# Two tiles of a down product as 2x2 blocks with seven block products

## The chip, the cores and the metric

The kernel runs on one core of a Trainium2 chip. A core has TensorE (matmuls, which write to PSUM), VectorE, ScalarE and GpSimd (elementwise work) and SyncE, whose queue issues most DMAs. Each engine takes its instructions in the order of the program and waits at an instruction until what it needs is there. The metric is the device time of one execution in microseconds (us). In the profile PE is TensorE, DVE is VectorE, ACT is ScalarE, POOL is GpSimd and SP is SyncE.

## The reference

The input x has 2 x 2048 rows of 1024 numbers, all fp32. Each row is normalised, and two things are made of it: `s`, a sum of six rolled copies of the row, where the rolls are the six largest lags of its autocorrelation and the weights their softmax; and `g`, a gated feed-forward layer whose weights are tiled four times and carry a small low-rank (LoRA) part.

```python
xn = _layernorm(x)
corr = irfft(f * conj(f)), f = rfft(xn)
weights, delay = top_k(corr, 6)
s = sum over k of softmax(weights)[k] * roll(xn, -delay[k])
gate = silu(qlora(xn, w1q, a1, b1))          # 1024 -> 2752
up = qlora(xn, w3q, a3, b3)
g = silu(qlora(gate * up, w2q, a2, b2))      # 2752 -> 1024
out = x + s * g
```

Since w2q is tiled four times, gate * up can be summed over its four quarters first: 688 numbers per row, five chunks of 128 and a rest of 48.

## The kernel before

The 4096 rows are taken in eight macro blocks of 512 rows, each of four tiles of 128 rows. For a macro block the feed-forward layer is done in 15 steps, written out by hand (`plan`, L648). Steps 0 to 9 are the **up stage**: chunk c (two steps per chunk) has four quarters j, each with a gate and an up product of 512 columns into two PSUM accumulators (L544), seeded by ScalarE with the LoRA part (`seed`, L522, L515), then a Silu on ScalarE (L549), a multiply on VectorE (L551) and a sum over the quarters on GpSimd (L554, L556) into `zf[c]`. Step 10 is the rest (`up_rest`: L573 and L580, Silu L590, multiply L591, sums L595 to L597). Steps 11 to 14 are the **down stage**, one tile of 128 rows each: `down` multiplies the five chunks of `zf` with the two halves of w2 (512 columns each, L620), then adds a short product of 64 rows with the rest and the LoRA part (L631); `out` takes Silu (L642), multiplies with `s` (L643), adds x (L644) and stores (L645). `lora_mid` (L599) prepares the LoRA part of the short product in step 11 (L604).

Between these products the program puts the work of the correlation for the **next** macro block. `pre`, `mid`, `half` and `end` are lists of what is issued at four places of a step, and `sums` gives how many of the weighted rolled copies are added at two of them:

- norm of tile r (`norm`, L183) in steps 0, 2, 4, 6: ScalarE normalises, VectorE makes `a` and folds it (L192, L143, L144), GpSimd makes `b` and folds it (L194, L132, L133). `turn` (L206) transposes the folds on TensorE (L216) about two steps later.
- powers of the spectrum (`power`, L388) in steps 9 and 10: TensorE, then ScalarE copies and squares (L395, L396, L381), VectorE multiplies (L382), GpSimd adds (L383, L386).
- `lags` and `search` of tile r (L405, L435) in steps 11 to 14: TensorE (L414), ScalarE (L418, L432), VectorE (L425 to L449), GpSimd (L450).
- gathers: GpSimd issues an indirect DMA per rolled copy (L474), VectorE adds it with its weight into `s` (L491; the first of six is a ScalarE product, L488). In the settled blocks step 14 adds one, in the first block three.

PSUM accumulators of the products and of the down stage come from one pool of five (`full`, L93), handed out in turn: a new one is free when the readers of the one five before it have done. Other tiles in SBUF have one to three buffers per tag: `e2` and `o2` (squares) one each, `x2` (the x tile for the output) and `g` two each.

Of the kernel before, what the change touches and what calls it, by code (L numbers as in the profile page):

```python
# [35 lines left out]
F32 = mybir.dt.float32  # L36
# [5 lines left out]
L = 1024  # L42
# [5 lines left out]
P = 128  # L48
# [20 lines left out]
def block_kernel(ctx: ExitStack, tc: tile.TileContext, x, w13t, w0t, w5t, w2t, a13, b13, b5, a2t, tf, ti, pick, out):  # L69
# [12 lines left out]
    p5 = pool("p5", ROLLS)  # L82
    small = pool("small", 3)
# [23 lines left out]
    w2_sb = const.tile([P, NC, L], F32)  # L107
    b5_sb = const.tile([P, 4], F32)
# [20 lines left out]
    def fold_b(b, bcs):  # L129

        at = lambda first, par, n: bass.AP(b.tensor, b.offset + first, [list(b.ap[0]), [par, 2], [n, P]])
        nc.gpsimd.tensor_tensor(bcs[:, 0:2, :], at(0, 1, 2), at(512, -1, -2), ALU.subtract)  # L132
        nc.gpsimd.tensor_tensor(bcs[:, 2:4, :], at(2, -1, 2), at(510, 1, -2), ALU.add)  # L133
# [12 lines left out]
    def fold_lora(nat):  # L146

        pairs = p1.tile([P, 2, 8, 4], F32, tag="e2", name="a_pairs")
        nc.gpsimd.tensor_tensor(pairs, nat[:, 0], nat[:, 1], ALU.add)
        nc.gpsimd.memset(a13_sb, 0.0)  # L150
        whole = p1.tile([P, 8, 4], F32, tag="o2", name="a_whole")
        nc.gpsimd.tensor_tensor(whole[:, :2], pairs[:, 0, :2], pairs[:, 1, :2], ALU.add)
        nc.gpsimd.tensor_tensor(whole[:, 2:], pairs[:, 0, 2:], pairs[:, 1, 2:], ALU.subtract)
        nc.scalar.activation(a13_sb[:, :, :4], whole, AF.Copy, scale=0.125)


    class Corr:
# [25 lines left out]
        def norm(self, r, tags=("yc", "bcs")):  # L183
# [6 lines left out]
            yc = p1.tile([P, 4, P], F32, tag=tags[0], name=f"yc_{n}")  # L190
            bcs = p1.tile([P, 4, P], F32, tag=tags[1], name=f"bcs_{n}")
            nc.vector.tensor_tensor(a, xt[:, :512], xt[:, 512:], ALU.add)  # L192
            fold_a(a, yc, rest)
            nc.gpsimd.tensor_tensor(b[:, :512], xt[:, :512], xt[:, 512:], ALU.subtract)  # L194
# [43 lines left out]
        def lora_spread(self):  # L238
# [6 lines left out]
            self.u = p1.tile([P, NR], F32, tag="u", name=f"u_{self.m}")  # L245
# [79 lines left out]
        def lora_first(self, ffn):  # L325
# [3 lines left out]
            self.u = p1.tile([P, NR], F32, tag="u", name=f"u_{m}")  # L329
# [10 lines left out]
            for g, tags in enumerate((("ec", "e2"), ("zf2", "zf3"))):  # L340
                e = full(f"fe_{m}_{g}")
                self.wave(e, g, 0)
                ec, e2 = [p1.tile([P, NR], F32, tag=tag, name=f"{tag}_{m}_{g}") for tag in tags]
                nc.scalar.copy(ec, e)
                nc.scalar.activation(e2, e, AF.Square)
                parts.append((ec, e2))
# [7 lines left out]
            nc.vector.tensor_copy(self.u, acc)  # L354
# [19 lines left out]
        def squares(self, g, ec, e2, o):  # L374
# [5 lines left out]
            o2 = p1.tile([P, NR], F32, tag="o2", name=f"o2_{m}_{g}")  # L380
# [7 lines left out]
        def power(self, g):  # L388
# [4 lines left out]
            ec = p1.tile([P, NR], F32, tag="ec", name=f"ec_{m}_{g}")  # L393
            e2 = p1.tile([P, NR], F32, tag="e2", name=f"e2_{m}_{g}")
# [10 lines left out]
        def lags(self, r):  # L405
# [13 lines left out]
            corr = p1.tile([P, L], F32, tag="corr", name=f"corr_{n}")  # L419
# [74 lines left out]
    class Ffn:  # L494
# [114 lines left out]
        def down(self, r, mid, half):  # L609
            row = (self.m * RT + r) * P  # L610
            xs = []
            for d in range(2):
                xt = p2.tile([P, 512], F32, tag="x2", name=f"x2_{self.m}_{r}_{d}")
                nc.sync.dma_start(xt, x[row : row + P, d * 512 : (d + 1) * 512])
                xs.append(xt)
            accs = [full(f"y_{self.m}_{r}_{d}") for d in range(2)]
            rc = slice(r * P, (r + 1) * P)
            for d, acc in enumerate(accs):
                for c in range(FULL):
                    nc.tensor.matmul(  # L620
                        acc, lhsT=self.zf[c][:, rc], rhs=w2_sb[:, c, d * 512 : (d + 1) * 512], start=(c == 0), stop=False
                    )
                if d == 0:
                    if r == 0:
                        self.lora_mid()
                    mid()
                    half()

            for d, acc in enumerate(accs):
                at = slice(64 * d, 64 * d + 64)  # L630
                nc.tensor.matmul(  # L631
# [304 lines left out]
```

## Time and profile before

| | |
|---|---|
| median of three runs | 1165.69 us (1164.72 to 1165.73) |
| the profiled execution | 1167.36 us, span of its instructions 1165.6 us |
| mean granted TensorE clock | 0.994 |
| DMA | 201.78 MB, mean 173 GB/s |
| first down-stage matmul of the eight macro blocks | 144.9, 294.3, 433.9, 573.5, 713.1, 852.7, 992.3, 1118.2 us |

The profile is of one execution. Its parts are: busy time of each engine; groups of instructions by line, with the shape (partitions x elements), the count, the busy time, the mean duration of one in ns and the idle time of the engine before them with what ended it; timelines, with start and duration in us; and windows, which give the busy time of each engine in a stretch of time. A matmul in fp32 appears as two records that overlap, so its duration is not its pace; the distance between starts is. Idle time of an engine that is not the bound costs nothing.

### The profile page before, as it was taken

The numbers are of one execution on the slowest core, as the hardware profiler recorded it, in microseconds if no ns is written. First come the engines' busy times: TensorE is split into PE (matmuls) and PEld (weight loads), VectorE is DVE, ScalarE is ACT, GpSimd is POOL, SyncE is SP. The second block draws the span as 40 slices with busy tenths as digits, with TensorE's granted clock in tenths as the row PEclk, the third lists the DMA queues.
The fourth block names the chain that finished last, engine by engine and source line by source line (L and its number), as shares of the span: only waits on it lengthen the run. The fifth ranks groups of instructions, "written<-read, shape, count | busy, mean of one in ns | idle before, by whom it ended". The sixth has DMA issues, their size and how long they took to land.

```text
span 1165.6 us, 11210 instructions
## 1 busy us (share of the span) xinstructions
PE 1138.2 (98%) x3540; PEld 485.7 (42%) x3540; DVE 755.3 (65%) x1009; ACT 603.7 (52%) x1045; POOL 814.4 (70%) x675
## 2 busy tenths in 40 slices
PE   5999999999999999999999999999999999999997
PEld 4344344343444434444344433444344443444432
DVE  5587488665586746865577656785658765573455
ACT  4656623666346662566535664266633666344531
POOL 4778767877577884777767776787866877564653
PEclk9999999899999999999999999999999999999999
DMA  9941368534565435654355443754357534452334
GB/s 364 372 151 75 109 203 293 184 132 145 163 214 183 142 130 180 217 181 162 128 175 201 169 160 109 236 207 147 118 157 237 181 127 155 144 190 90 119 116 162
DMA packets 64915, 201.78 MB, mean 173 GB/s; under 512 B 7612, under 2 KB 7868, under 8 KB 64088
## 3 DMA queue, kind: packets, MB, share of 16 engines
q0 software_dynamic: 27648, 100.68, 26.9%
q1 hardware_dynamic: 37208, 100.39, 23.9%
q8 instruction: 28, 0.46, 0.2%
q14 instruction: 31, 0.25, 0.1%
HBM read 150.65 MB, written 50.39 MB: 172 GB/s over the span
## 4 chain that ended last, share of the span: by engine, by line
PE 87%; DVE 7%; POOL 2%; ACT 2%; issue 2%; DMA 0%; DVEq 0%; ACTq 0%; POOLq 0%
PE gu L544 44%; PE y L620 21%; PE u L527 4%; PE y L631 3%; PE gu L580 2%; PE t L216 2%; PE gu L573 2%; DVE s L491 1%; PE fe L369 1%; PE fe L372 1%; PE fo L369 1%; PE o L414 1%; PE fo L372 1%; PE ua L232 1%; PE e L414 1%
## 5 line engine op out<-in xcount | busy, mean ns | idle before, releaser
L544 PE MATMUL gu<-yT,w_sb 128*128 128x512 f32 x960 | 460.5, 601 | 0.1
L620 PE MATMUL y<-w_sb,zf 128*128 128x512 f32 x640 | 287.5, 597 | 0.5 <-ACT g L642 0.5
L544 PEld LDWEIGHTS gu<-yT,w_sb 128*128 128x128 f32 x960 | 176.8, 191 | 233.9 <-issue 214.4
L474 POOL DMA_INDIRECT roll<-scr,lag x192 | 230.2, 1199 | 47.4 <-issue 33.3
L491 DVE SCALAR_TENSOR_TENSOR s<-roll,w,s 128x1024 f32<-128x1024 f32 x160 | 249.0, 1556 | 7.2 <-DMA roll<-scr,lag 4.3
L551 DVE TENSOR_TENSOR z<-z,gu 128x512 f32<-128x512 f32 x160 | 109.2, 683 | 175.9 <-PE gu L544 118.0
L522 ACT ACTIVATE gu<-second,b_sb 128x512 f32<-128x512 f32 x320 | 207.6, 684 | 10.2 <-DVE z L551 9.3
L549 ACT ACTIVATE z<-gu 128x512 f32<-128x512 f32 x160 | 95.3, 596 | 177.8 <-PE gu L544 176.2
L620 PEld LDWEIGHTS y<-w_sb,zf 128*128 128x128 f32 x640 | 117.3, 190 | 147.8 <-issue 144.7
L644 POOL TENSOR_TENSOR g<-g,x 128x512 f32<-128x512 f32 x62 | 101.8, 1661 | 94.2 <-DVE g L643 88.5
L544 PE MATMUL gu<-yU,w_sb 128*128 128x512 f32 x320 | 163.8, 593 | 0.0
L556 POOL TENSOR_TENSOR zf<-zf,z 128x512 f32<-128x512 f32 x80 | 127.8, 1598 | 21.5 <-DVE z L551 20.3
L554 POOL TENSOR_TENSOR zf<-z,z 128x512 f32<-128x512 f32 x40 | 51.8, 1295 | 85.9 <-DVE z L551 84.2
L544 PEld LDWEIGHTS gu<-yU,w_sb 128*128 128x128 f32 x320 | 61.1, 191 | 77.2 <-issue 73.6
L643 DVE TENSOR_TENSOR g<-s,g 128x512 f32<-128x512 f32 x64 | 41.6, 690 | 67.5 <-ACT g L642 67.4
L450 POOL TENSOR_TENSOR e<-euler,e 128x6 f32<-128x6 f32 x32 | 45.8, 1431 | 41.8 <-DVE e L449 40.0
L642 ACT ACTIVATE g<-y 128x512 f32<-128x512 f32 x64 | 34.8, 593 | 77.3 <-PE y L631 59.6
L432 ACT COPY corr<-corr 128x511 f32<-128x511 f32 x32 | 19.8, 619 | 79.7 <-DVE corr L431 79.7
L527 PE MATMUL u<-z,a_sb 128*2 128x512 f32 (+1 forms) x384 | 52.9, 591 | 2.0 <-DVE z L551 2.0
L143 DVE SCALAR_TENSOR_TENSOR yc<-a,rest 128x256 f32<-128x256 f32 x28 | 41.6, 1487 | 5.3 <-POOL rest L188 2.0
L515 ACT ACTIVATE gu<-second,b_sb 64x512 f32<-64x512 f32 x64 | 43.9, 686 | 1.7
L418 ACT COPY oc<-o 128x258 f32<-128x258 f32 x32 | 12.0, 375 | 63.0 <-PE o L414 62.8
(167 smaller groups left out, 1358.9 us busy)
## 6 DMA issues: line engine op xcount, KB each, us to landing
scr<-x SPq DMA_DIRECT2D x64, 512.0 KB
x<-in_x SPq DMA_DIRECT2D x32, 512.0 KB
x<-in_x SPq DMA_DIRECT2D x64, 256.0 KB
out<-g SPq DMA_DIRECT2D x64, 256.0 KB
w_sb<-in_w13t SPq DMA_DIRECT2D x5, 1024.0 KB
second<-rows SPq DMA_DIRECT2D x14, 256.0 KB
w_sb<-in_w2t SPq DMA_DIRECT2D x1, 3072.0 KB
roll<-scr,lag POOLq DMA_INDIRECT x192, 5.7
```

What stands on the lines that cost most here:

```text
L450: nc.gpsimd.tensor_tensor(e, bass.AP(euler.tensor, euler.offset, [list(euler.ap[0]), [0, TOP]]), e, ALU.pow)
L474: nc.gpsimd.indirect_dma_start(out=g, out_offset=None, in_=st.scratch[r].rearrange("p (n o) -> (p n) o", o=1), in_offset=bass.IndirectOffs ...
L491: nc.vector.scalar_tensor_tensor(s, g, w, s, ALU.mult, ALU.add)
L522: nc.scalar.activation(acc, self.st.second[:, wi, :], AF.Copy, scale=b13_sb[:, c, q : q + 1])
L527: nc.tensor.matmul(self.u2[32 * j : 32 * j + 2, :], lhsT=a2_sb[:rows, 4 * c + j, :], rhs=z[:rows, :], start=(c == 0), stop=(c == FULL),)
L544: nc.tensor.matmul(acc, lhsT=w13_sb[:, c, 2 * j + wi, k, :], rhs=y, start=False, stop=(k == 1), skip_group_check=True,)
L549: nc.scalar.activation(z, accs[0], AF.Silu)
L551: nc.vector.tensor_tensor(z, z, accs[1], ALU.mult)
L554: nc.gpsimd.tensor_tensor(self.sum_of(c), zs[0], zs[1], ALU.add)
L556: nc.gpsimd.tensor_tensor(self.zf[c], self.zf[c], z, ALU.add)
L620: nc.tensor.matmul(acc, lhsT=self.zf[c][:, rc], rhs=w2_sb[:, c, d * 512 : (d + 1) * 512], start=(c == 0), stop=False)
L644: (nc.vector if last else nc.gpsimd).tensor_tensor(g, g, xs[d], ALU.add)
```

## The change

Two tiles (i = 0, 1; `q` counts the pairs) are taken together in the down stage. The first four chunks of `zf` are named by two numbers: chunk 2a + k. The product of a pair over these chunks is one of 2x2 blocks: rows i, inner index k, column halves n, where each block product is a sum over a (two matmuls). A scheme after Strassen and Winograd makes it from seven block products instead of eight:

- Once, in the first macro block, GpSimd forms four combinations of w2 (`mix_weights`, 1024 elements each): T1 (in place of a block of w2), T2, T3, T4.
- Per macro block GpSimd forms four combinations of `zf` for a = 0 at the end of step 8 and for a = 1 at the end of step 9 (`mix`): S1, S2, S4 in buffers of the norm (`a`, `yc`, `bcs`) and A10 replaced in place by A00 - A10.
- A pair takes two steps. `down_head` makes p1, copies it on ScalarE into a second accumulator, makes p7, copies that to SBUF, adds p6 to p1, and VectorE writes p1 + p6 + p7 to a third; then p2 and the plain chunk 4. `down_tail` adds p5, VectorE writes that plus p7 to the fourth, and p4, p3, the plain chunks and the short products follow. All four accumulators are held from the head on. Outputs of the first half are issued in the middle of the tail.
- In `norm` the subtraction for `b` and both its folds go from GpSimd to VectorE.
- `px`, a pool of three buffers under one tag `x2`, holds the squares `e2` and `o2`, the x tiles of the output, and the finished output, which is now written over the x tile. The fourth x tile of a pair is loaded after the first output. `ec` goes to the two `g` buffers, `corr` to that of `cT`, `u` to that of `us`.
- The sums of rolled copies are dealt out anew: step 12 one instead of three, step 14 three instead of one (settled blocks); in the first block similar. The seeds of the next macro block move to the middle and the end of the last step.

```diff
     def fold_b(b, bcs):
...
-        nc.gpsimd.tensor_tensor(bcs[:, 0:2, :], at(0, 1, 2), at(512, -1, -2), ALU.subtract)
-        nc.gpsimd.tensor_tensor(bcs[:, 2:4, :], at(2, -1, 2), at(510, 1, -2), ALU.add)
+        nc.vector.tensor_tensor(bcs[:, 0:2, :], at(0, 1, 2), at(512, -1, -2), ALU.subtract)
+        nc.vector.tensor_tensor(bcs[:, 2:4, :], at(2, -1, 2), at(510, 1, -2), ALU.add)
...
+    B = lambda k, n: w2_sb[:, :4, :].rearrange("p (a k) l -> p a k l", k=2)[:, :, k, n * 512 : (n + 1) * 512]
+    T1, T2, T3, T4 = B(0, 1), t_sb[:, 0], t_sb[:, 1], t_sb[:, 2]
+    mix_weights = [
+        lambda: nc.gpsimd.tensor_tensor(T3, B(1, 1), B(0, 1), ALU.subtract),
+        lambda: nc.gpsimd.tensor_tensor(T1, B(0, 1), B(0, 0), ALU.subtract),
+        lambda: nc.gpsimd.tensor_tensor(T2, B(1, 1), T1, ALU.subtract),
+        lambda: nc.gpsimd.tensor_tensor(T4, B(1, 0), T2, ALU.subtract),
+    ]
...
             nc.vector.tensor_tensor(a, xt[:, :512], xt[:, 512:], ALU.add)
+            nc.vector.tensor_tensor(b[:, :512], xt[:, :512], xt[:, 512:], ALU.subtract)
             fold_a(a, yc, rest)
-            nc.gpsimd.tensor_tensor(b[:, :512], xt[:, :512], xt[:, 512:], ALU.subtract)
             fold_b(b[:, :], bcs)
...
-            o2 = p1.tile([P, NR], F32, tag="o2", name=f"o2_{m}_{g}")
+            o2 = px.tile([P, NR], F32, tag="x2", name=f"o2_{m}_{g}")
...
+        def mix(self, a):
...
+            S1, S2, S4 = [t[:, 2 * a : 2 * a + 2, :] for t in self.S]
+            A = lambda i, k: self.zf[2 * a + k].rearrange("p (q i n) -> p q i n", q=2, i=2)[:, :, i, :]
+            nc.gpsimd.tensor_tensor(S1, A(1, 0), A(1, 1), ALU.add)
+            nc.gpsimd.tensor_tensor(S2, S1, A(0, 0), ALU.subtract)
+            nc.gpsimd.tensor_tensor(A(1, 0), A(0, 0), A(1, 0), ALU.subtract)
+            nc.gpsimd.tensor_tensor(S4, A(0, 1), S2, ALU.subtract)
...
+        def down_head(self, q, mid, half):
...
+            for i, n in ((0, 0), (1, 0), (0, 1)):
+                self.load_x(i, n)
...
+                    (A(0, 0), B(0, 0)), (A(0, 1), B(1, 0)), (S[2], B(1, 1)), (A(1, 1), T4), (S[0], T1), (S[1], T2), (A(1, 0), T3),
...
+            self.ys = [full(f"y_{self.m}_{2 * q + i}_{n}") for n in range(2) for i in range(2)]
+            y00, y10, y01, y11 = self.ys
+            self.add_to(y01, p1_, True)
+            nc.scalar.copy(y00, y01)
+            self.add_to(y11, p7_, True)
+            self.p7 = p5.tile([P, NR], F32, tag="z", name=f"p7_{self.m}_{q}")
+            nc.scalar.copy(self.p7, y11)
+            self.add_to(y01, p6_)
+            nc.vector.tensor_tensor(y10, y01, self.p7, ALU.add)
+            if q == 0:
+                self.lora_mid()
+            mid()
+            half()
+            self.add_to(y00, p2_)
+            self.add_to(y00, self.plain(0, 0))
+
+        def down_tail(self, mid, half, s, between):
...
+            self.add_to(y01, p5_)
+            nc.vector.tensor_tensor(y11, y01, self.p7, ALU.add)
+            mid()
+            half()
+            self.add_to(y10, p4_)
+            self.add_to(y10, self.plain(1, 0))
+            self.rest(0, (y00, y10))
+            self.out(0, 0, y00, s)
+            self.load_x(1, 1)
+            self.out(1, 0, y10, s)
+            between()
+            self.add_to(y01, p3_)
+            self.add_to(y01, self.plain(0, 1))
+            self.add_to(y11, self.plain(1, 1))
+            self.rest(1, (y01, y11))
+            self.out(0, 1, y01, s)
+            self.out(1, 1, y11, s)
...
+            (nc.vector if last else nc.gpsimd).tensor_tensor(xt, g, xt, ALU.add)
+            nc.sync.dma_start(out[row : row + P, cols], xt)
...
-        sums[8], sums[9], sums[11], sums[14] = (2, 1), (2, 1), (1, 0), (1, 0)
+        sums[7:10] = [(2, 1)] * 3
+        sums[11:] = [(1, 0), (1, 0), (2, 1), (3, 0)]
+        between = lambda: None
         if first:
-            sums = [(0, 0)] * 7 + [(1, 1), (2, 1), (1, 1), (2, 2), (2, 2), (2, 1), (2, 1), (3, 0)]
+            sums = [(0, 0)] * 7 + [(1, 1), (2, 1), (1, 2), (2, 2), (2, 1), (1, 0), (2, 1), (3, 0)]
+            for p, f in enumerate(mix_weights):
+                half[6 + p].append(f)
...
-            mid[STEPS - 1].insert(0, lambda: (ffn_next.seed(0), ffn_next.seed(1, (0,))))
+            mid[STEPS - 1].insert(0, lambda: ffn_next.seed(0, (0,)))
+            between = lambda: (ffn_next.seed(0, (1,)), ffn_next.seed(1, (0,)))
             end[STEPS - 1].insert(0, lambda: ffn_next.seed(1, (1,)))
+        for a in range(2):
+            end[8 + a].append(lambda a=a: ffns[m].mix(a))
```

## The prediction

> **What bounds the kernel now.** I read the page first (busy shares), then TensorE's own waits, then one macro block (rows 1536 to 2047, the fourth) engine by engine. TensorE is the bound nearly everywhere:
>
> ```profile
> PE 1138.2 (98%) x3540; PEld 485.7 (42%) x3540; DVE 755.3 (65%) x1009; ACT 603.7 (52%) x1045; POOL 814.4 (70%) x675
> ```
>
> A busy TensorE need not be a fast one, so I looked at the pace. Each fp32 matmul of 128x512 appears as two records, and inside a run of them the starts are 0.429 us apart: ten records of L620 start at 573.48 and the next ten at 585.27 and so on, always 4.46 us for ten. One matmul is 0.858 us. Three groups, and the windows of the down stage (573.5 to 617.4) and of the following up stage (busy us of TensorE, its weight loads, VectorE, ScalarE, GpSimd; then the granted clock):
>
> ```profile
> L620 PE MATMUL y<-w_sb,zf 128*128 128x512 f32 x640 | 287.5, 597 | 0.5 <-ACT g L642 0.5
> L386 POOL TENSOR_TENSOR bT<-bT 128x1024 f32<-128x1024 f32 x8 | 19.8, 2469 | 0.6
> L383 POOL TENSOR_TENSOR bT<-e,o 128x512 f32<-128x512 f32 x16 | 20.3, 1270 | 3.0 <-ACT o L381 2.5
> ```
>
> ```profile
> 573.50:617.40 43.90, 43.90 (x137) 19.54 (x135) 29.80 (x46) 12.72 (x23) 26.12 (x20) 1.00 0.59 190
> 617.40:713.10 95.70, 95.70 (x301) 39.57 (x300) 62.72 (x79) 62.80 (x108) 75.51 (x65) 1.00 0.47 160
> ```
>
> To be seen: in a settled macro block (139.6 us from one to the next) TensorE has no idle time at all. Whatever the others take is hidden today; the question is only whether it stays so. TensorE's real waits are few: 9.2 us at the start, then 1.2, 2.0, 1.9, 0.5 and 2.6 us, all before 210 us.
>
> **What is removed.** Per macro block the old down product takes 40 matmuls of 128 rows; the new one takes, per pair of tiles, seven products of two matmuls and four plain ones, 36 in all. The short ones (L631) stay 8, in the same concurrent pairs. Eight blocks x 4 x 0.858 = **-27.5 us**, wholly on TensorE's path.
>
> **What is added off TensorE, costed by rows.** Per pair: two ACT copies (L395, a copy out of PSUM, 0.58 us) and two VectorE adds with a PSUM operand (L551, 0.68 us): 19 and 22 us over the kernel. Per half block `mix` puts four 256-element adds on GpSimd. No row shows that size undisturbed; 512 elements take 1.27 (L383) and 1024 some 2.4 (L386), so a straight line gives 0.7, with the 0.08 us between dependent adds 0.8, **3.2 us** per `mix`; ends 2.5 (half of 1.27 each) and 4.1 (L133 beside a busy VectorE, 1.03). I take 3.2. Against that the fold of b leaves GpSimd: 1.28 + 0.91 + 1.03 = 3.2 us x 28 = 90 us less. On VectorE it costs 0.69 + 0.42 + 0.42, but a and yc, now 0.69 + 1.51 + 1.07 beside the GpSimd folds, should fall to the 0.69 + 0.50 + 0.42 of the first block's undisturbed rows, so VectorE's norm goes from 3.3 to 3.1 us. As sums none of this binds. But four new orders are laid across queues, and each has to be checked where it sits.
>
> **Wait 1, start of the down stage.** Before, tile 0 needed one free accumulator at once and one 4.4 us later. Now the first product goes to the third accumulator allotted (`y01`), which is the one of the second group of the rest (`gu_5_1`) and is free only after its VectorE multiply (L591). The timelines of GpSimd, ScalarE, VectorE and TensorE before that point:
>
> ```profile
> 550.70 1.27 POOL L554 TENSOR_TENSOR zf<-z,z 128x512 f32<-128x512 f32 x1 [1.30 <-DVE z L551]
> 556.26 1.27 POOL L556 TENSOR_TENSOR zf<-zf,z 128x512 f32<-128x512 f32 x1 [1.29 <-DVE z L551]
> 559.38 3.21 POOL L386 TENSOR_TENSOR pwy<-pwy,cT 128x1024 f32<-128x1024 f32 x1
> 566.31 1.28 POOL L556 TENSOR_TENSOR zf<-zf,z 128x512 f32<-128x512 f32 x1
> 567.53 1.26 POOL L383 TENSOR_TENSOR bT<-e,o 128x512 f32<-128x512 f32 x1
> ...
> 569.33 0.59 ACT L381 ACTIVATE o<-fo 128x512 f32<-128x512 f32 x1
> ...
> 570.67 1.30 DVE L591 TENSOR_TENSOR z<-z,gu 64x512 f32<-64x512 f32 x2
> ...
> 573.48 4.46 PE L620 MATMUL y<-w_sb,zf 128*128 128x512 f32 x10
> ```
>
> Today L591's second ends at 571.97, 1.5 us before it would be needed. The first `mix` comes after the add at 550.70, the second after the one at 566.31. GpSimd's idle time between takes part of the first: L386 starts 0.9 late. The second is in full, so the add at 567.53 ends at 573.1 instead of 568.8. Of the shared tag `x2` (three buffers) the last square `o2` takes the buffer that this add frees, and ScalarE runs in order: `o2` starts at 573.1 instead of 569.33, and behind it are queued the four Silu of the rest, then the copies of the LoRA rows, then the new copy of `y01`. L591's second ends 2.64 us after `o2` starts, at 575.8: TensorE waits up to 2.3 us. With the cheap end of `mix` it is 1.1; I take **2.1 us** x 6 blocks = +12.6. The last block has no powers and waits for nothing here. In the first block the four weight sums (1024 elements, 2.4 us each) lie on GpSimd too, and there L591's second already ends 3.3 us after the point where TensorE would now need it (148.2 against 144.9): I take 4.5, less the 1.9 us wait of the short product there, which goes because that product moves back: **+2.6**.
>
> **Wait 2, inside the down stage.** The product into `y01` must wait until VectorE has read it twice. The first reading has 3 us of room. The second (`y11`) is queued behind a search (3.0 us), up to two gather sums (1.28 each) and a lag fold (0.95), and the search comes late by what delayed GpSimd. Laying VectorE's rows in order from 576 gives `y11` ready within 0.2 us of need for the first pair and 0.5 us late for the second. Ends 0 and 2; I take **0.6** x 7 = +4.2.
>
> **Wait 3, start of the next up stage.** The last step now has three sums ahead of the output multiplies. A Silu needs one of two `g` buffers, which GpSimd's add frees, so the last two Silu, the multiplies, the search and then L551 move back; the last x tile is loaded only when the first output has left its buffer, (on SP that load waits for the first store to land, and the second store behind it), and GpSimd stands at its add with the power of the next weights and `rstd` behind it, for which ScalarE's norm waits. The first block already ends with three sums, so the row is there: its successor starts at 192.45 and its first L551 at 201.84, 9.4 us after, against 4.85 us in the settled block; and the transposes stall:
>
> ```profile
> 209.01 0.66 PE L216 MATMUL t<-ident,yc 128*128 128x128 f32 x2 [2.56 <-DVE yc L143]
> 209.91 0.69 PE L216 MATMUL t<-ident,yc 128*128 128x128 f32 x2 [0.24 <-DVE yc L144]
> ...
> 622.32 0.68 DVE L551 TENSOR_TENSOR z<-z,gu 128x512 f32<-128x512 f32 x1
> ...
> 631.31 0.60 PE L216 MATMUL t<-ident,yc 128*128 128x128 f32 x4
> ```
>
> In the settled block the last fold of b ends at 631.07, 0.2 us ahead of the transposes, so there is no room. Ends 0 and 2.8, the measured stall. The norm in one queue ends 0.9 us sooner than 4.0 us (627.04 to 631.07); the x load gives back about half a us. I take **2.4** x 6 = +14.4, the first boundary having its stall already.
>
> **Ends.** The last output waits for its late x tile: about +0.6.
>
> **The clock.** The trace shows what an idle TensorE costs afterwards:
>
> ```profile
> 92.60:96.00 3.40, 1.45 (x5) 0.34 (x5) 3.30 (x8) 3.40 (x7) 2.21 (x4) 1.00 0.00 0
> 96.00:99.40 3.40, 3.40 (x11) 2.31 (x10) 3.36 (x6) 1.78 (x4) 2.11 (x2) 0.50 0.00 0
> 154.00:157.40 3.40, 1.88 (x5) 0.57 (x3) 3.26 (x5) 0.00 (x0) 2.27 (x3) 1.00 1.03 308
> 208.60:215.50 6.90, 6.25 (x13) 3.29 (x14) 5.85 (x9) 4.09 (x9) 6.63 (x6) 0.51 0.56 179
> ```
>
> An idle 1.95 us was followed by 3.4 us at half clock (1.7 us lost), 2.56 us by 6.8 us (3.4 lost), one of 1.87 us, cut by the edge of a 3.4 us stretch, by none. The Trainium skill ("TensorE: Matmul & The Clock Gate", the part on HAM oscillation) says instead that only idle gaps over about 3.4 us let the clock fall. By that rule waits of 2.1 and 2.4 us cost nothing more; by the rows each may cost 1.7 to 3.4. The rows decide; since the stretch is cut at times that don't follow the kernel, and a slow TensorE shortens the next wait, I take three falls of 1.7: **+5.1**.
>
> **Sum.** -27.5 + 12.6 + 2.6 + 4.2 + 14.4 + 0.6 + 5.1 = **+12.0**. The profiled execution took 1167.36 us (span 1165.6 and 1.8 around it), so it would be 1179.4; it lies 1.7 above the median of the runs, 1165.69, so for the runs I say **1178**. Without the clock it is 1173.
>
> **Rivals.** (1) *The waits stay hidden.* If `mix` costs 2.5 and GpSimd, 90 us lighter, has caught up, wait 1 is 0.7, wait 2 nothing, wait 3 0.7: 4.2 + 1.5 + 4.2 + 0.6 = 10.5 us against 27.5, so **1149**; 1140 to 1158. For it: GpSimd's 26 us of 43.9 in the down stage and VectorE's 30. It decides if the second `mix` ends before about 569.5. Against it: GpSimd has no idle time from 559.4 to 577.8. Chance 0.27. (2) *Gain and waits cancel*, 1163 to 1168: 0.09. (3) *The clock falls at every wait*: 13 waits at up to 3.4 us, 44 us in place of 5.1: **1217**; 1192 and more. For it the row at 208.6; against it the one at 154. Chance 0.12. That fewer matmuls are not fewer TensorE microseconds I leave out: the pace is even. My own case has 0.52, 1166 to 1192.
>
> **Numbers.** Measurement tells about 0.2% (2.3 us) from no change. Faster: rival 1 and a little of mine, 0.28; within 0.2%: 0.09; slower: 0.63. A tenth left out at each end, in rivals 1 and 3, gives 1147 to 1200.
>
> **What would show it.** L620's successors with 576 records of 0.429 us; idle time of TensorE before the first of them in each down stage, released by VectorE's multiply; GpSimd's add of the third power ending some 4 us later against TensorE; idle time before the first transposes; clock windows at 0.5 after them. I am wrong if the block period is under 138 us: then `mix` was absorbed, or the accumulators come free in another order than I counted.

## The result and the profile after

The changed kernel takes **1177.14 us** (median; 1176.3 to 1179.55) against 1165.71 for the kernel before beside it: ratio 1.0103, 95% interval 1.0085 to 1.012. The profiled execution has a span of 1177.7 us against 1165.6, so 12.1 us have to be found, and with the 27.5 us of matmuls that are gone, 39.6 us of something new.

In the changed kernel the first block deals out only 22 of its 24 sums of rolled copies. Every later block then runs two places behind in the list: its fourth tile is stored before its last two copies are added, and the last two of all are never added. Every run below on the changed kernel has this too, unless its text says that it has 24. The prediction did not see it. What it is worth in time is measured below, with the late load of x out of the way (`x4_24`); for the changed kernel as it stands it was not measured.

First the page: busy time of each engine (us, share of the span, instructions) and the groups that bear on the change (busy us, mean ns of one, then idle time ahead of them and what ended it).

```profile
PE 1120.5 (95%) x3476; PEld 472.5 (40%) x3476; DVE 758.2 (64%) x1122; ACT 619.5 (53%) x1077; POOL 779.3 (66%) x659
...
L503 DVE SCALAR_TENSOR_TENSOR s<-roll,w,s 128x1024 f32<-128x1024 f32 x158 | 237.1, 1501 | 17.5 <-DMA roll<-scr,lag 14.9
...
L724 POOL TENSOR_TENSOR x<-g,x 128x512 f32<-128x512 f32 x62 | 84.9, 1379 | 72.2 <-DMA x<-in_x 46.4
L641 PE MATMUL y<-w_sb,zf 128*128 128x512 f32 x256 | 121.4, 596 | 0.0
...
L641 PE MATMUL y<-t_sb,zf 128*128 128x512 f32 x128 | 64.0, 624 | 5.7 <-DVE z L603 5.7
...
L641 PE MATMUL y<-w_sb,S 128*128 128x512 f32 x128 | 61.9, 606 | 2.0 <-DVE y L698 2.0
```

The product has its 576 records (256 + 128 + 128, and 64 more of another operand), TensorE 64 fewer in all: 32 matmuls are gone as counted. But at `L724`, the add of x, GpSimd has stood idle 46.4 us for loads of x. In the kernel before the same add had 5.5:

```profile
L644 POOL TENSOR_TENSOR g<-g,x 128x512 f32<-128x512 f32 x62 | 101.8, 1661 | 94.2 <-DVE g L643 88.5 <-DMA x<-in_x 5.5
```

Now the windows of one settled block, its down stage and the up stage after it (busy us of TensorE, its weight loads, VectorE, ScalarE, GpSimd; then the granted clock):

```profile
583.00:624.65 41.65, 41.04 (x129) 17.88 (x127) 31.97 (x53) 16.61 (x31) 25.73 (x20) 1.00 0.58 187
624.65:724.25 99.60, 97.49 (x300) 40.61 (x299) 60.73 (x89) 60.88 (x105) 67.99 (x61) 0.98 0.47 159
```

From its first product to the first of the up stage the down stage became shorter, 43.99 us (573.48 to 617.47) to 41.65. The up stage, whose products nobody touched, went from 95.6 to 99.6 us, with 2.1 us of idle TensorE and a clock of 0.98. So the loss lies behind the product, not in it. TensorE's waits over the whole execution (us in total, times, longest):

```profile
PE t L230 <- DVE yc L145: 15.2, 6, 3.0
...
PE y L641 <- DVE z L603: 5.7, 1, 5.7
PE y L641 <- ACT y L681: 3.6, 6, 0.6
```

The first row is the transposes at the start of the up stage, the second the new product p7 in the first block, the third the new product p6 in six settled blocks. Smaller ones, 2.0 us at L641 for the add L698 and 1.8 at L426, lie in the first block. Put against the prediction's terms (sums of the trace's waits and of the time at half clock, the stretch after the last matmul left out of the latter; a stretch at half clock counts half):

| term | predicted | measured |
|---|---|---|
| matmuls removed | -27.5 | -27.5 |
| start of the down stage, settled blocks | +12.6 | +3.6 (6 x 0.61) |
| waits in the first block | +2.6 | +8.7 (5.2 to 13.9, the transposes after it included) |
| inside the down stage | +4.2 | 0 in settled blocks |
| start of the up stage | +14.4 | +12.5 (2.20, 2.99, 2.11, 2.69, 2.50) |
| end, after the last matmul | +0.6 | +3.5 (6.8 to 10.35) |
| clock | +5.1 | +6.8 (10.2 us at half clock before, 23.9 after) |
| waits before the first block's down stage | 0 | +1.6 |
| rest, in no wait; 0.5 us a settled down stage are starts further apart | 0 | +2.9 |
| sum | +12.0 | +12.1 |

The sum is right and its parts are not; the experiments ask why.

**Start of the down stage.** The timeline of GpSimd, ScalarE, VectorE and TensorE (start, duration, engine and line; in brackets idle time before and its releaser):

```profile
580.07 0.72 POOL L636 TENSOR_TENSOR S<-zf,S 128x256 f32<-128x256 f32 x1
580.75 1.26 POOL L395 TENSOR_TENSOR bT<-e,o 128x512 f32<-128x512 f32 x1
...
582.05 0.60 ACT L393 ACTIVATE o<-fo 128x512 f32<-128x512 f32 x1 [3.25 <-POOL bT L395]
582.54 2.03 ACT L602 ACTIVATE z<-gu 64x512 f32<-64x512 f32 x4
...
586.78 0.57 ACT L681 COPY y<-y 128x512 f32<-128x512 f32 x1
...
583.40 2.52 DVE L603 TENSOR_TENSOR z<-z,gu 64x512 f32<-64x512 f32 x4
...
583.01 1.88 PE L641 MATMUL y<-w_sb,zf 128*128 128x512 f32 x4
584.84 1.96 PE L641 MATMUL y<-t_sb,zf 128*128 128x512 f32 x4
587.40 1.98 PE L641 MATMUL y<-t_sb,S 128*128 128x512 f32 x4 [0.61 <-ACT y L681]
```

The chain is there link by link: `mix` (last add L636), the held add L395, the square L393 that waits 3.25 us for it, the Silu and the multiply L603, whose second instruction ends at 583.40 + 2 x 0.63 = 584.66. But the product that needs it is p7, at 584.84, and not p1, which starts at 583.01, before the first of these multiplies. So it comes 0.2 us in time, and the one wait left is p6 for the copy of `y01` at the end of ScalarE's queue.

**Start of the up stage**, same block (SPq is SyncE's queue):

```profile
626.65 0.34 SPq L725 DMA_DIRECT2D out<-x  x1
630.79 0.33 SPq L659 DMA_DIRECT2D x<-in_x  x1
...
634.06 1.27 POOL L724 TENSOR_TENSOR x<-g,x 128x512 f32<-128x512 f32 x1 [4.32 <-DMA x<-in_x]
635.29 1.35 POOL L462 TENSOR_TENSOR e<-euler,e 128x6 f32<-128x6 f32 x1
636.63 0.54 POOL L191 TENSOR_TENSOR rstd<-var,mhalf 128x1 f32<-128x1 f32 x1
...
637.57 1.24 ACT L200 ACTIVATE x<-x,shift,rstd 128x1024 f32<-128x1024 f32 x1 [3.09 <-POOL shift L193]
...
640.15 0.48 DVE L145 SCALAR_TENSOR_TENSOR yc<-a,rest 128x256 f32<-128x256 f32 x1
...
640.77 1.06 PE L230 MATMUL t<-ident,yc 128*128 128x128 f32 x4 [2.11 <-DVE yc L145]
```

SyncE issues the store of the first output at 626.65 and the load of the fourth x tile only at 630.79, when that store has left the buffer (in SyncE's waits, `SPq L659 <- DMA out<-x: 54.5, 25, 3.9`: 54.5 us in 25 loads). GpSimd stands 4.32 us at its last add for this tile, with the power for the softmax weights (L462) and `rstd` of the next norm (L191) queued behind; ScalarE's norm waits 3.09 us for those, VectorE's folds for the norm, and the transposes 2.11 us for the folds.

**Clock.** Windows right after the transposes' waits of 2.99 and 2.11 us, and then after that of 2.50 us; the clock is the third number from the end:

```profile
500.90:504.20 3.30, 3.30 (x5) 1.24 (x4) 3.30 (x4) 2.15 (x6) 3.13 (x2) 0.50 0.42 158
640.90:644.20 3.30, 3.30 (x11) 2.26 (x12) 3.30 (x7) 2.63 (x6) 1.82 (x1) 0.50 0.94 322
924.70:928.00 3.30, 3.30 (x14) 1.76 (x15) 3.30 (x7) 2.82 (x7) 1.75 (x1) 1.00 0.91 320
```

The wait of 2.69 us is like the first two, that of 2.20 us like the last. So three waits were followed by 3.41 us at half clock, two by none.

### The profile page after: what moved, and what is told of

Same layout as the page of the kernel before. It is cut to its first block, busy times and chain, and to the rows that moved or that the text cites. A ratio compares the mean times of both kernels' runs of the same rounds, so it can differ in the third digit from the quotient of the medians.

```text
span 1177.7 us, 11263 instructions
## 1 busy us (share of the span) xinstructions
PE 1120.5 (95%) x3476; PEld 472.5 (40%) x3476; DVE 758.2 (64%) x1122; ACT 619.5 (53%) x1077; POOL 779.3 (66%) x659
## 4 chain that ended last, share of the span: by engine, by line
PE 50%; POOL 19%; DMA 11%; issue 9%; ACT 6%; DVE 4%; SPq 0%; POOLq 0%; DVEq 0%; ACTq 0%
PE gu L556 37%; POOL roll L486 5%; DMA x<-in_x 5%; DMA out<-x 4%; PE y L641 3%; POOL x L724 3%; PE u L539 3%; PE t L230 2%; DMA roll<-scr,lag 2%; POOL e L462 2%; ACT gu L527 2%; POOL bT L395 1%; POOL zf L568 1%; PE fe L381 1%; PE fo L381 1%
## 5 line engine op out<-in xcount | busy, mean ns | idle before, releaser
L486 POOL DMA_INDIRECT roll<-scr,lag x192 | 240.1, 1250 | 51.4 <-issue 30.5
L503 DVE SCALAR_TENSOR_TENSOR s<-roll,w,s 128x1024 f32<-128x1024 f32 x158 | 237.1, 1501 | 17.5 <-DMA roll<-scr,lag 14.9
L724 POOL TENSOR_TENSOR x<-g,x 128x512 f32<-128x512 f32 x62 | 84.9, 1379 | 72.2 <-DMA x<-in_x 46.4
L641 PE MATMUL y<-w_sb,zf 128*128 128x512 f32 x256 | 121.4, 596 | 0.0
L566 POOL TENSOR_TENSOR zf<-z,z 128x512 f32<-128x512 f32 x40 | 57.9, 1447 | 85.8 <-DVE z L563 85.7
L462 POOL TENSOR_TENSOR e<-euler,e 128x6 f32<-128x6 f32 x32 | 46.7, 1461 | 69.0 <-DVE e L461 69.0
L723 DVE TENSOR_TENSOR g<-s,g 128x512 f32<-128x512 f32 x64 | 55.2, 885 | 39.0 <-ACT g L722 37.6
L641 PEld LDWEIGHTS y<-w_sb,zf 128*128 128x128 f32 x256 | 46.9, 191 | 57.9 <-issue 57.0
L641 PE MATMUL y<-t_sb,zf 128*128 128x512 f32 x128 | 64.0, 624 | 5.7 <-DVE z L603 5.7
L641 PE MATMUL y<-w_sb,S 128*128 128x512 f32 x128 | 61.9, 606 | 2.0 <-DVE y L698 2.0
L206 DVE TENSOR_TENSOR a<-x 128x512 f32<-128x512 f32 x28 | 33.1, 1183 | 26.7 <-ACT x L200 26.7
```

The source lines that it names most:

```text
L462: nc.gpsimd.tensor_tensor(e, bass.AP(euler.tensor, euler.offset, [list(euler.ap[0]), [0, TOP]]), e, ALU.pow)
L486: nc.gpsimd.indirect_dma_start(out=g, out_offset=None, in_=st.scratch[r].rearrange("p (n o) -> (p n) o", o=1), in_offset=bass.IndirectOffs ...
L503: nc.vector.scalar_tensor_tensor(s, g, w, s, ALU.mult, ALU.add)
L566: nc.gpsimd.tensor_tensor(self.sum_of(c), zs[0], zs[1], ALU.add)
L641: nc.tensor.matmul(acc, lhsT=lhs, rhs=rhs, start=(first and a == 0), stop=True, skip_group_check=True)
L724: (nc.vector if last else nc.gpsimd).tensor_tensor(xt, g, xt, ALU.add)
```

## The experiments

Times are medians; each ratio is to the kernel before, run beside it, with its 95% interval. All edits are to the changed kernel, except `fold_only`. The question was what delays the transposes: the three sums of the last step (my weightier reason) or GpSimd standing for the late x tile (in my working "about half a us").

### x4_early: the fourth x tile loaded early

```diff
# down_head, after the first products
+            self.load_x(1, 1, p5, "z")
# down_tail, after the first output
-            self.load_x(1, 1)
```

> The changed kernel with the fourth x tile of a pair loaded already in the head, into a buffer of the z tag that is free then, instead of after the first output. Theory A (the three sums of step 14 make the search late, and GpSimd's wait for x is only the last 1.1 us of it): the waits before the first transposes fall from 2.1 to 3.0 us to about 1.0 to 1.9, no clock falls there, the end of the kernel is 3.5 us shorter; about 1161 us. Theory B (GpSimd's 4.3 us wait for x, with the power and rstd behind it, makes the whole wait): the waits are gone; about 1155 us.

Measured: 1158.12 us, ratio 0.9939 (0.9915 to 0.9962). The same place in its timeline:

```profile
619.34 1.27 POOL L724 TENSOR_TENSOR x<-g,x 128x512 f32<-128x512 f32 x1 [0.68 <-issue]
622.16 1.35 POOL L462 TENSOR_TENSOR e<-euler,e 128x6 f32<-128x6 f32 x1 [1.54 <-DVE e L461]
...
625.33 1.24 ACT L200 ACTIVATE x<-x,shift,rstd 128x1024 f32<-128x1024 f32 x1 [1.93 <-POOL shift L193]
...
628.53 0.69 PE L230 MATMUL t<-ident,yc 128*128 128x128 f32 x4 [0.36 <-DVE yc L145]
```

GpSimd no longer waits for x, but for the search; the transposes wait 0.35 to 0.39 us instead of 2.1 to 3.0, the clock falls after none of them, and five settled blocks take 138.1 us each instead of 141.2 in the mean. The stretch after the last matmul goes from 10.35 to 8.6 us. With the three sums still in place, 0.36 us is all that they and everything else leave: the late x tile was the cause. (The edit also takes this tile out of the shared pool of three buffers; the run does not separate that from the earlier load.)

### sums_back: the sums where the kernel before had them

```diff
-        sums[11:] = [(1, 0), (1, 0), (2, 1), (3, 0)]
+        sums[11:] = [(1, 0), (2, 1), (2, 1), (1, 0)]
```

> The changed kernel with three sums in step 12 and one in step 14 in the settled blocks, as the kernel before has them. Theory A: the waits before the first transposes are gone in the five settled blocks, with the falls of the clock there, the end stays; about 1160 us. Theory B: the waits stay at 2.1 to 3.0 us; about 1177 us. In both VectorE could reach the first reading of y01 of the second pair late, by up to 1.3 us a block.

Measured: 1184.47 us, ratio 1.0161 (1.0135 to 1.0187). The transposes' waits went to between 0 and 0.8 us in the settled blocks, but not because the norm came sooner: the x add comes 53.7 us after the block's first product instead of 51.1. TensorE itself comes later. Two products inside the down stage now wait in every block like this:

```profile
616.90 1.98 PE L641 MATMUL y<-w_sb,S 128*128 128x512 f32 x4 [1.29 <-DVE y L686]
625.43 1.98 PE L641 MATMUL y<-w_sb,S 128*128 128x512 f32 x3 [2.02 <-DVE y L698]
```

These are the adds that turn `y01` into `y10` and `y11`. They stand on VectorE behind the sums that moved, the second also behind 1.7 us in which VectorE waits for the first, scaled copy of a tile on ScalarE (L500); TensorE waits 0.3 to 1.3 us and 2.0 us. That is the prediction's wait 2, and the place of the sums in the changed kernel is what keeps it away.

### mix_late: the second mix later

```diff
-        for a in range(2):
-            end[8 + a].append(lambda a=a: ffns[m].mix(a))
+        end[8].append(lambda: ffns[m].mix(0))
+        mid[10].insert(0, lambda: ffns[m].mix(1))
```

> The changed kernel with the second mix of a block issued in the middle of step 10, before the fourth power, so that GpSimd adds the third power first. If the wait of 0.6 us before p6 comes from o2 waiting for GpSimd behind that mix, it is gone in six blocks (3.6 us), and the first block's wait of 5.7 us falls by about 3: about 1170 us. If it comes from the four copies of the LoRA rows that stand before the copy of y01 on ScalarE, nothing changes: 1177 us.

Measured: 1178.52 us, ratio 1.0112 (1.0089 to 1.0136). The 0.61 us of p6 are gone from the settled blocks, two waits of 0.23 and 0.25 us are new. In the first block p7 now waits 2.84 us for the late `mix` itself and a later product 3.90. No gain: with only 0.6 us waited at this place, little was to be had.

### fold_only: the kernel before with the folds of b on VectorE

```diff
-        nc.gpsimd.tensor_tensor(bcs[:, 0:2, :], at(0, 1, 2), at(512, -1, -2), ALU.subtract)
-        nc.gpsimd.tensor_tensor(bcs[:, 2:4, :], at(2, -1, 2), at(510, 1, -2), ALU.add)
+        nc.vector.tensor_tensor(bcs[:, 0:2, :], at(0, 1, 2), at(512, -1, -2), ALU.subtract)
+        nc.vector.tensor_tensor(bcs[:, 2:4, :], at(2, -1, 2), at(510, 1, -2), ALU.add)
...
+            nc.vector.tensor_tensor(b[:, :512], xt[:, :512], xt[:, 512:], ALU.subtract)
-            nc.gpsimd.tensor_tensor(b[:, :512], xt[:, :512], xt[:, 512:], ALU.subtract)
```

> The kernel before with only b and its folds moved to VectorE. By the prediction's sum VectorE's norm takes 3.1 us instead of 3.3 and the fold of b ends 0.9 us sooner: nothing to gain in settled blocks, the one wait of 2.8 us before the second block's transposes falls to about 1.9 and perhaps its half clock goes: 1161 to 1165 us. Rival: VectorE comes late with multiplies and seeds and the settled blocks get new waits: 1168 us or more.

Measured: 1160.61 us, ratio 0.9964 (0.9953 to 0.9975). The settled blocks stay at 139.61 us to the hundredth. Of the 6.9 us between the two profiled executions, 5.1 are at the one place where the kernel before waited for a norm: the transposes after its first block wait 1.1 us instead of 2.8, and the clock does not fall after them (6.83 us at half clock there before).

### fold_back: the changed kernel with the folds back on GpSimd

The reverse of the edit above, on the changed kernel.

> The changed kernel with b and its folds back on GpSimd. From the prediction's rows the norm then ends 0.9 us later (4.0 instead of 3.1) and GpSimd takes 3.2 us more per tile: the waits before the first transposes grow from 2.1 to 3.0 to some 3 to 4 us in five blocks and the clock falls at each: about 1187 us. Rival: the fold on VectorE only moves work and gives nothing inside this change: 1177 us.

Measured: 1191.91 us, ratio 1.0229 (1.0204 to 1.0254), 14.8 us above the changed kernel. TensorE's waits at the transposes, and the clock after one of them:

```profile
PE t L230 <- DVE yc L145: 18.1, 6, 3.3
...
PE t L230 <- DVE yc L146: 2.7, 6, 0.5
```

```profile
506.95:510.30 3.35, 3.30 (x7) 1.66 (x7) 3.35 (x4) 2.36 (x5) 3.18 (x3) 0.50 0.32 124
```

Waits of 3.2 to 3.8 us at each of the five settled boundaries, and after every one the clock falls. So the same move that is worth nothing in a settled block of the kernel before is worth 14.8 us once the norm is on the path.

### weights_early: the four combinations of w2 in steps 2 to 5

```diff
-                half[6 + p].append(f)
+                half[2 + p].append(f)
```

> The changed kernel with the four combinations of w2 formed in steps 2 to 5 of the first block instead of 6 to 9. If GpSimd's queue (weights, then mix, then the third power that o2 waits for) makes the 5.7 us wait before p7 in the first block, it falls by the 2.4 us of the weight sum that stands right before the third power, to about 3.3, and the block's later waits shrink with it: about 1173 us. If the two sums on VectorE ahead of the multiply of the rest make it, it stays at 5.7: 1177 us. The settled blocks stay as they are in both.

Measured: 1177.77 us, ratio 1.0099 (1.0075 to 1.0122). In the first block p7's wait falls from 5.7 to 1.2 us, but three waits of about 1 us appear in the first up stage and others of 2.8 and 2.1 us in the down stage and at the seeds. The load moved along GpSimd's queue and stayed on the path.

### x4_lora: the copies of the LoRA rows behind the start of the down stage

With x early; ScalarE's copies that stand ahead of the copy of `y01` are issued in the middle of the step.

```diff
-            pre[11].extend([nxt.again, nxt.lora_spread])
+            mid[11].extend([nxt.again, nxt.lora_spread])
```

> The kernel with the early fourth x tile, and the copies of yT and of the LoRA rows (2.3 us of ScalarE) moved from ahead of the pair's head to behind p6. The 0.6 us wait before p6 comes from the copy of y01 standing behind them, so it should go in six blocks: 3.6 us less than with the early x tile alone, about 1154.5 us. If the copy is late for another reason, 1158 us.

Measured: 1212.65 us, ratio 1.041 (1.039 to 1.0429). TensorE's waits:

```profile
PE e L426 <- ACT yU L269: 42.0, 7, 9.1
PE y L641 <- DVE z L603: 11.4, 7, 6.5
```

The copies are the readers of a PSUM bank that the lags (L426) need: 5.5 us of idle TensorE in each block, with the clock at half for 6.8 us beside it. The second row bears on the prediction: with p6 no longer held up, the settled blocks show 0.8 us of waiting for L603, the multiply that I had named for the start of the down stage. The mechanism exists, at p7.

### x4_all: the same, with the combinations of w2 early and 24 sums

```diff
+            sums = [(0, 0)] * 6 + [(0, 1), (2, 1), (2, 1), (2, 2), (1, 1), (2, 1), (2, 0), (2, 1), (3, 0)]
...
+                half[2 + p].append(f)
...
+            mid[11].extend([nxt.again, nxt.lora_spread])
```

> The same with the weights of w2 formed in steps 2 to 5 and the first block dealing out all its 24 sums, from step 6 on (the changed kernel deals out 22 there, so that each block's last tile is stored before its last two copies are added and the last two are never added). The first block's waits of 11.8 us and its half clock of 10.2 us shrink to about a third: about 1147 us. If the sums on VectorE make the first block late, not GpSimd, about 1153 us.

Measured: 1215.72 us, ratio 1.0427 (1.0408 to 1.0445): the same 5.5 us, and 1.66 us before the transposes on top. It decides nothing about its parts.

### x4_between: the copies right behind the copy of y01

```diff
+            if q == 0:
+                self.turned()
...
+            ffns[m].turned = lambda: (nxt.again(), nxt.lora_spread())
```

> The early fourth x tile, and the copies of yT and of the LoRA rows issued right after the copy of y01 instead of before it (their matmul then follows the first product). The copy of y01 no longer stands behind 2.3 us of copies: the 0.6 us wait before p6 goes in six blocks, while nothing waits for the accumulator of the LoRA rows: about 1154.5 us. If the accumulators of the down stage are the real limit, p7 waits for the multiply of the rest instead, up to 0.8 us, as when those copies were moved further back: about 1159 us.

Measured: 1158.28 us, ratio 0.9947 (0.993 to 0.9965), a settled block 138.18 us. The 0.61 us of p6 are gone, 0.23 and 0.25 us come in its place, and the block is as long as with x early alone: the wait was not the last limit there.

### x4_wdve: the combinations of w2 on VectorE

```diff
-        lambda: nc.gpsimd.tensor_tensor(T3, B(1, 1), B(0, 1), ALU.subtract),
+        lambda: nc.vector.tensor_tensor(T3, B(1, 1), B(0, 1), ALU.subtract),
# and T1, T2, T4 alike; x early
```

> The early fourth x tile, and the four combinations of w2 formed on VectorE at their old places (about 1.3 us each there instead of 2.4). GpSimd's queue in the first block is then 2.4 us shorter just ahead of the third power, VectorE has room in that stretch: the 5.7 us wait before p7 falls to about 3 and one window of half clock goes: about 1154 us. If VectorE's own queue makes that wait, it stays or grows: 1158 us or more.

Measured: 1154.02 us, ratio 0.9909 (0.9891 to 0.9926). The first block takes 149.7 us instead of 153.7: p7's wait is 2.0 us instead of 5.7. It was GpSimd's queue that carried the combinations, and taking them off it does what shifting them did not.

### x4_24: all 24 sums of a block

With x early; the two left-out sums are added at the ends of steps 6 and 7 of the first block.

```diff
-            sums = [(0, 0)] * 7 + [(1, 1), (2, 1), (1, 2), (2, 2), (2, 1), (1, 0), (2, 1), (3, 0)]
+            sums = [(0, 0)] * 6 + [(0, 1), (1, 2), (2, 1), (1, 2), (2, 2), (2, 1), (1, 0), (2, 1), (3, 0)]
```

> The early fourth x tile, and the two sums that the changed kernel leaves out of the first block dealt out there at the ends of steps 6 and 7, so that every tile is stored after all its copies are added. Two more sums of 1.3 us are nothing in a kernel whose VectorE is 64% busy; but all later sums stand two places earlier in their block. If that is without effect, 1158 us; if the last step's three sums then end later against the outputs, the waits before the transposes grow from 0.4 to about 1.6 us in five blocks: 1164 us.

Measured: 1169.28 us, ratio 1.0041 (1.0025 to 1.0057), 11 us more than `x4_early`, 139.5 us a settled block. The two sums are some 3 us of VectorE once; a settled block adds 24 copies either way, and only which copies fall in which step has shifted by two. VectorE's and ScalarE's timeline in the third step of the down stage:

```profile
607.97 1.14 ACT L500 ACTIVATE s<-roll,w 128x1024 f32<-128x1024 f32 x1
...
609.14 2.61 DVE L503 SCALAR_TENSOR_TENSOR s<-roll,w,s 128x1024 f32<-128x1024 f32 x2 [1.74 <-ACT s L500]
```

With the complete list the fourth tile begins here, and its first copy is a ScalarE product that stands behind the copies of a lag; VectorE stands 1.74 us for it, and the transposes wait 1.66 us, 27 us later. That the second follows from the first was not followed link by link.

### full_dealt: a version that beats both

24 sums, x early, the combinations of w2 on VectorE, and that first ScalarE product moved to the end of the step before, which also leaves two sums instead of three in the last step.

```diff
-        sums[11:] = [(1, 0), (1, 0), (2, 1), (3, 0)]
+        sums[11:] = [(1, 0), (1, 1), (2, 1), (2, 0)]
```

> The changed kernel with the fourth x tile loaded early, the weight sums on VectorE, and all 24 sums of a block (the first block's two left-out ones added at the ends of its steps 6 and 7). In the run that had the 24 sums without the last edit, VectorE waited 1.74 us in the third step of the down stage for ScalarE's first scaling of the fourth tile's weighted sum (L500), which sits behind other copies, and the transposes then waited 1.66 us. Here that first scaling is moved to the end of the step before, and the step with the last outputs has two sums instead of three. If that scaling, and not the number of sums, is what the complete dealing costs, the waits before the transposes fall back below 0.5 us, a settled block takes 138.1 us again and the kernel 1154 to 1158 us. If the scaling only moves the stall to the end of the step before (ScalarE then stands for VectorE's output multiply, and the copy of y01 behind it), the product p6 or the sum y10 waits 1 to 2 us instead, a settled block takes 139 to 140 us and the kernel 1163 to 1168 us.

Measured: **1151.17 us** (1150.74 to 1151.89), ratio 0.9876 (0.9857 to 0.9895). From its page, waits and the two windows of a settled block:

```profile
L503 DVE SCALAR_TENSOR_TENSOR s<-roll,w,s 128x1024 f32<-128x1024 f32 x160 | 241.6, 1510 | 4.1 <-DMA roll<-scr,lag 2.3
...
L724 POOL TENSOR_TENSOR x<-g,x 128x512 f32<-128x512 f32 x62 | 83.2, 1358 | 30.7 <-DVE g L723 24.9
```

```profile
PE y L641 <- ACT y L681: 3.6, 8, 1.1
...
PE t L230 <- DVE yc L145: 2.7, 6, 0.8
```

```profile
567.90:609.10 41.20, 40.87 (x129) 17.87 (x127) 32.27 (x53) 15.99 (x30) 25.36 (x19) 1.00 0.59 203
609.10:705.60 96.50, 96.13 (x300) 39.44 (x299) 61.31 (x88) 60.79 (x105) 67.43 (x62) 1.00 0.46 159
```

All 160 VectorE sums are there, the x add waits for its own product and no longer for a load, and a settled block takes 137.7 us, with 0.7 us of waits and the clock at 1.00. Of 3.43 us that the product saves per block 1.9 now reach the end (139.6 to 137.7). The waits before the transposes are back to 0.35 to 0.44 us, but the run does not tell whether the moved ScalarE product did it or the two sums in place of three.

Of the 14.6 us against the kernel before, some 5 may be had without the seven products, by moving the folds alone (`fold_only`). The 1.9 us of a settled block are not among them, since `fold_only` leaves that block as it was. So the seven products do pay; what ate them was the rest of the rearrangement.

## Why the prediction was right in its sum and where its steps failed

**Matmuls removed: right.** 32 matmuls, at the pace read off before. (The groups of ten were read loosely: the second starts at 579.83, and every other one takes 4.56 us. The 0.429 us between starts hold.) Of the 3.4 us per block, about 0.5 us is lost again to starts a little further apart in the down stage (-2.34 us for the stage in place of -3.43 + 0.61).

**Wait 1: mechanism right, place wrong.** 2.1 us x 6 was predicted, 0.61 x 6 found. The step that failed is "the first product goes to the third accumulator allotted (`y01`), which is the one of the second group of the rest": the accumulators come free in another order than I counted, which the last paragraph named as a way to be wrong. p1 starts before any of the four multiplies of the rest, in the first block even before their Silu (142.66 against 145.41), so `y01` has none of the rest's four accumulators. p7 waits for the second multiply, 1.83 us later, so that one is `y11`. This fits buffers that are handed out in the order of first use (`y01`, `y00`, `y11`, `y10`) and not in that of the list in the code, by which I had applied the rule of "the one five before it". The square started 0.96 us ahead of the first product where I had 0.4, in part because `mix` took 2.9 us and not 3.2. Those two leave a margin of 0.2 us; the wait that is left is at the end of the same ScalarE queue.

**First block: the mis-sized term.** +2.6 was predicted; without its matmuls the block cost 12.0 more (from its first product to the next block's 158.0 us and not 149.4, so 8.6 longer, with 3.4 us fewer of matmuls). "I take 4.5" for the one wait was near, 5.69 us measured. What the step lacked is in this timeline:

```profile
144.92 0.60 ACT L393 ACTIVATE o<-fo 128x512 f32<-128x512 f32 x1 [7.27 <-POOL bT L395]
...
146.15 2.60 DVE L503 SCALAR_TENSOR_TENSOR s<-roll,w,s 128x1024 f32<-128x1024 f32 x2
148.78 2.52 DVE L603 TENSOR_TENSOR z<-z,gu 64x512 f32<-64x512 f32 x4
...
150.23 3.75 PE L641 MATMUL y<-t_sb,zf 128*128 128x512 f32 x4 [5.69 <-DVE z L603]
...
165.08 0.71 PE L426 MATMUL o<-ti_sb,bT 128*128 128x129 f32 x4 [1.80 <-ACT oc L430]
...
173.75 1.98 PE L641 MATMUL y<-w_sb,S 128*128 128x512 f32 x4 [1.71 <-DVE y L698]
```

The square waits 7.27 us behind GpSimd's queue, and two sums stand on VectorE ahead of the multiplies; a late block then runs into three more waits of 1.5 to 1.8 us, and its down stage has 10.2 us at half clock (5.1 us lost). The late x tile has 4.3 of these 12 us (158.0 to 153.7 in `x4_early`), the combinations of w2 in GpSimd's queue 4.0 (`x4_wdve`).

**Wait 2: not there.** 0.6 x 7 was predicted; the settled blocks have none, the first block 2.0 us. The room was there, but `sums_back` shows how little: with the sums moved ahead of these adds, they cost up to 1.3 and 2.0 us in every settled block.

**Wait 3: size right, its causes weighed wrongly.** The chain from the late x tile through GpSimd's add to the norm was named, its weight was not. 2.4 us was predicted, 2.1 to 3.0 found. I had taken it from the stall after the first block of before ("The first block already ends with three sums"), and put the x load at half a microsecond. `x4_early` leaves the sums, loads x early, and 2.1 of the 2.5 us are gone. The row I leant on had another reason too: `fold_only` takes 1.7 of its 2.8 us with the folds alone. I also counted six boundaries where five are left: the last block has no next norm.

**End: mis-sized.** +3.5 us, not +0.6. The same chain of store and load has nothing behind which to hide in the last block: the first output's store is issued at 1167.95, the load at 1169.96, and the last add, for which VectorE stands 2.7 us, comes at 1173.70. That is only part of it: with x early the stretch is still 8.6 us (`x4_early`), so the late load has 1.7 of the 3.5, and the rest was not taken apart.

**Clock: right about the rule.** +5.1 was predicted, +6.8 found: three falls in the settled blocks as taken, the rest in the first block. That it was three of the five waits, I could not know. The rule of the Trainium skill ("TensorE: Matmul & The Clock Gate", HAM oscillation) that gaps over about 3.4 us are what lets the clock fall would have given none of these; the waits of 2.11, 2.69 and 2.99 us each had one. The fall after 1.95 us at 96 us in the kernel before is absent in the changed one, with the same wait of 1.95 us in the same place: such a wait is at the edge.

**The total** is right by luck: 15 us counted too much (9 at wait 1, 4 at wait 2, 2 at wait 3) stood against 15 counted too little (6 in the first block, 3 at the end, 2 of clock and 4.5 of small things). Rival 1 (1149 us, the waits hidden) is near `full_dealt` with 1151, which has the waits taken away but the weight sums on VectorE too (4 us in `x4_wdve`). In the changed kernel rival 1 failed on the x tile, not on what I let it hang on, the end of the second `mix`: that came late, 2.2 us before the first product, and cost 0.6 us.

## What to carry to other kernels

When buffers are shared to make room, follow the load into a buffer that comes free late, and then everything queued behind the instruction that waits for it; here one load of 256 KB per pair, issued 18 us after the other three, cost more than half of what 32 matmuls saved. A stall seen in one block of a trace is a size for another block only if its cause is the same: test it with one edit before leaning on it. Work taken off a hidden engine is worth nothing until a chain through that engine sets the end, and then it is worth a lot (0 us a settled block before, 14.8 us in all after).

## What the runs showed of the hardware that was not expected

**Falls of the clock lie on a grid.** The prediction had taken from its rows that the stretches are cut at times that don't follow the kernel. The runs show how. Each fall lasts 3.41 us or twice that (10.24 us once, in `x4_lora`). In the changed kernel they begin at 149.29, 166.36, 217.56, 500.86, 640.81 and 784.17 us; the distances are 5, 15, 83, 41 and 42 times 3.413 us. In another execution the grid lies elsewhere: `x4_early` has the wait of 5.69 us at the same place (to 150.16 us against 150.23), and its fall begins at 147.47.

`sums_back` shows what the place is worth. Each of its six settled down stages has a wait of 2.02 us. Three of these waits lie inside one stretch of its grid (they end at 482.82, 625.43 and 908.87 us, the stretches at 483.07, 626.43 and 909.74), and at each of these ends the clock falls. The other three are cut by a line of the grid, into 0.64 and 1.38, 0.48 and 1.54, 0.41 and 1.60 us, and after none of them does it fall. Windows after the wait to 625.43 and after the cut one to 767.92:

```profile
626.50:629.80 3.30, 3.30 (x6) 1.22 (x5) 2.08 (x3) 2.48 (x5) 2.97 (x3) 0.50 0.47 164
768.00:774.00 6.00, 6.00 (x15) 2.34 (x16) 3.18 (x7) 3.39 (x6) 5.48 (x5) 1.00 0.63 207
```

So the same wait costs 1.7 us more or nothing, by where it falls. In `fold_back` the blocks are 143.3 us long and 42 times 3.413 is 143.36, so every boundary meets the grid at nearly the same place, and the clock falls at every one (220.21, 363.57, 506.93 and on, 143.36 apart); its waits are longer too. The place is not all: in the changed kernel the wait of 2.50 us (to 924.64), cut into 1.98 and 0.53, had no fall, that of 2.99 us, cut into 1.23 and 1.77, had one. How much idle time within a stretch decides was not settled.
